# A four-layer graph network on one core: the engines' order by a list scheduler in the kernel, softmax in blocks of rows, scores as columns

## The chip, the cores and the metric

The kernel runs on one core of one Trainium2 chip. Five engines of the core matter here: TensorE (PE, matrix products and transposes, its weight loads shown apart as PEld), VectorE (DVE), ScalarE (ACT), GpSimd (POOL) and SyncE (SP, which here only issues transfers). The metric is the device time of one launch in microseconds (us), the median of three runs.

## The reference, cut to what matters

The input `x` holds 32 batches of 512 nodes by 128 features in float32; `adj` is one 512x512 matrix of zeros and ones that all batches and layers share. Four layers follow each other, each on the layer-normalised input with a residual:

```
for layer in (L0, L1, L2, L3):
    x = x + layer(relu(layernorm(x)))

L0: h = x @ Wo ; u1 = h @ a1 ; u2 = h @ a2
    e[i,k] = leaky(u1[idx1[i,k]] + u2[idx2[i,k]], 0.1)   # the indices of pairs are fixed
    att = softmax(where(adj > 0, e, -9e15), axis=1) ; out = att @ h + x @ Ws
L1: h = x @ Wp + bp ; s = leaky(h@a_src [:,None] + h@a_dst [None,:], 0.2)
    hg = relu(ln(softmax(where(A > 0, s, lowest)) * A @ h, g, b))
    z = relu(ln(((1 + eps) * hg + A @ hg) @ W1 + b1, mg, mb)) ; out = relu(z @ W2 + b2 + hg)
L2: h = x @ W ; e = leaky(h@a1 [:,None] + h@a2 [None,:], 0.2)
    out = elu(softmax(where(adj > 0, e, -9e15)) @ h + bias)
L3: A = softmax(where(adj > 0, e[cumsum index], -9e15))  # the same for every batch
    out = (A * I) @ (x @ W0) + (A * (1 - I)) @ (x @ W1) + bias
```

## The kernel before, in words

Everything stays in SBUF: `xs` holds all 32 batches (as 128 partitions by four chunks of 128 features each), loaded by SP `AHEAD = 8` batches ahead and overwritten by each layer's residual sum. One batch of one layer is a *chain*, written as a generator: `layer0` (L561), `layer1` (L636), `layer2` (L694), `layer3` (L713). A `yield` stands wherever the chain would wait. `interleave` (L40) steps through all chains that are under way, one stretch between two yields of each in turn, and lets a new one in after a number of steps, so that about `DEPTH = 6` are under way at a time. The generator `prepare` (L243), which makes what the later layers need once (score weights, centred weights, bias terms as bf16 triples, the transposed adjacency with 1 + eps on its diagonal, layer 3's softmax), is put in after two chains. The order on each engine follows from this program order and from which tile is free: scratch tiles come from pools (`wk` 18, `hp` 4 for projections, `yp` 3 for the 512x512 scores, `bg` 2 for transposed scores), and PSUM has 8 banks of 128x512.

All layers begin with `preln`: eight small statistics instructions on DVE, a power on POOL, four normalising instructions on POOL, then four PE transposes and a ReLU on ACT (`hT`, L464/466). `project_scored` (L493/497) multiplies by a weight with score columns appended (`w0_ext` 130 wide, `w1_ext` and `w2_ext` 129 wide) and copies the result to SBUF on ACT (`h_sc`).

Layers 1 and 2 share `attend` (L507). The row of neighbour scores, needed on every partition, comes from one 512-wide matmul with a weight whose score vector is repeated 128 times (`prow`, L512), so it needs only `hT`, not the projection. Four fused instructions on DVE add the mask and give the row maximum (`y`, `rmax`, L517), two small ones the shift `nmax`; ACT does the leaky ReLU (L529) and the exponential with its row sum (L530) for each block of 128 rows; after a `yield`:

```
for jb in range(C):
    pt = bank("pt")
    for ib in range(C):
        nc.tensor.transpose(pt[:, ib, :], y[:, ib, blk(jb)], ident)
```

A block of *columns* is transposed here (L539), so the first needs all four row blocks. The copies out of PSUM (`pT`) are on ACT and DVE alternately in layer 2 (L541, L543) and are DVE products with `adjT` in layer 1 (L545). Then sixteen 128x128 matmuls (`po`, L550).

Layer 0 works on transposed scores over half the nodes. After the projection, four small SP transfers gather the pair scores (`u`, L575), DVE makes `ls` (L568, L570) and `lt` (L579), PE spreads `ls` by four transposes (`repeated`, L504), DVE masks it (`y`, L588) and makes `top`, `nmax`, `ltn` (L595 to L601); ACT exponentiates (L604, L607); DVE makes `rs` and two scaled copies of h (L614 to L621); twenty matmuls (L626, L628) and the residual sum (L633) end it. Layer 1 goes on after `po` with a layer norm (POOL power L443), `hn` on DVE and POOL, the ReLU `hg` (L657, DVE), `pg` (L661, four 512-wide matmuls), `pz`, a second layer norm, transposes, `px` (L476) and two DVE instructions. Layer 2 ends with an elu (`em` L707 on ACT, then two on DVE, the last the sum into `xs`, L710). Layer 3 multiplies `hT` by one weight (`p`, L476), copies it (`h`, L724, ACT), takes the diagonal part (`own`, L717), does twenty matmuls (`po`, L728 and L732), adds and stores.

Of the kernel before, what the change touches and what calls it, by code (L numbers as in the profile page):

```python
# [23 lines left out]
F32 = mybir.dt.float32  # L25
# [5 lines left out]
P = 128  # L31
# [3 lines left out]
DEPTH = 6  # L35
# [4 lines left out]
def interleave(chains):  # L40


    waiting = list(chains)[::-1]
    running = []
    until = 0.0
    while waiting or running:
        if until <= 0.0 and waiting:
            chain, gap = waiting.pop()
            running.append(chain)
            until += gap  # L50
        until -= 1.0
        for chain in list(running):
            try:
                next(chain)
            except StopIteration:
                running.remove(chain)
# [3 lines left out]
def kernel(  # L60
# [33 lines left out]
    P1 = P + 1  # L94
# [3 lines left out]
    assert F == P and C == 4 and NE % P == 0 and B >= DEPTH  # L98
# [3 lines left out]

    def bank(name):
        return ps.tile([P, C, P], F32, tag="bank", name=name)
# [7 lines left out]


    W_O, W_S, W_P, W_1, W_2, W_L2, W_30, W_31 = range(8)
    wts = cp.tile([P, 8, P], F32, name="wts")
    att = cp.tile([P, 2], F32, name="att")
    a2 = cp.tile([P, 2], F32, name="a2")
    a1 = cp.tile([P, 3], F32, name="a1")
    e_col = cp.tile([P, KE], F32, name="e_col")
    e_last = cp.tile([P, 1], F32, name="e_last")  # L120
    eps_bc = cp.tile([P, 1], F32, name="eps_bc")
    mlp_gb = cp.tile([P, 2], F32, name="mlp_gb")
    G_G, G_B, B_2, B_L2, B_L3, B_P, B_1 = range(7)
    rows = cp.tile([P, 7, P], F32, name="rows")
    xs = cp.tile([P, B, C, P], F32, name="xs")

    bias = cp.tile([P, C, N], F32, name="bias")

    nc.scalar.dma_start(wts[:, W_O, :], l0_wo)
    nc.scalar.dma_start(att, l0_att.rearrange("(t p) o -> p (t o)", p=P))  # L130
    nc.scalar.dma_start(wts[:, W_S, :], l0_ws)
    for ib in range(C):
        nc.sync.dma_start(bias[:, ib, :], adj[blk(ib), :])

    def load_x(b):
        nc.sync.dma_start(xs[:, b], x[b].rearrange("(c p) f -> p c f", p=P))

    for b in range(AHEAD):
        load_x(b)
    for n, w in enumerate((l1_wp, l1_w1, l1_w2, l2_w, l3_w[0], l3_w[1])):  # L140
        nc.sync.dma_start(wts[:, W_P + n, :], w)
    nc.sync.dma_start(a2, l2_a.rearrange("(t p) o -> p (t o)", p=P))
    for n, v in enumerate((l1_asrc, l1_adst, l1_bp)):
        nc.sync.dma_start(a1[:, n : n + 1], v.rearrange("(p o) -> p o", o=1))
    nc.sync.dma_start(e_col, l3_e.rearrange("o (t p) -> p (o t)", p=P))
    nc.sync.dma_start(e_last, l3_e[:, NE - 1 : NE].to_broadcast([P, 1]))
    nc.sync.dma_start(eps_bc, l1_eps.rearrange("(a o) -> a o", o=1).to_broadcast([P, 1]))
    for n, v in enumerate((l1_mg, l1_mb)):
        nc.sync.dma_start(mlp_gb[:, n : n + 1], v.rearrange("(p o) -> p o", o=1))
    for n, v in enumerate((l1_gg, l1_gb, l1_b2, l2_bias, l3_bias, l1_bp, l1_b1)):  # L150
        nc.sync.dma_start(rows[:, n, :], v.rearrange("(o h) -> o h", o=1).to_broadcast([P, P]))


    ident = cp.tile([P, P], F32, name="ident")
    make_identity(nc, ident)
    mhalf = cp.tile([P, C], F32, name="mhalf")
    nc.vector.memset(mhalf, -0.5)
    minus1 = cp.tile([P, 1], F32, name="minus1")
    nc.vector.memset(minus1, -1.0)

# [43 lines left out]
    def score_weights(wn, a_cols, col, rep_src=None, rep=None):  # L204
# [8 lines left out]
        if rep is None:  # L213
            return
# [567 lines left out]
```

## Time and profile before

| what | value |
|---|---|
| median of three runs (lowest to highest) | 1177.77 us (1177.34 to 1178.57) |
| the profiled execution, its span, mean granted clock | 1178.93 us, 1177.1 us, 0.986 |
| PE `po` L550, 2048 matmuls | 243.8 us busy, mean 276 ns |
| PE `pg` L661, 256 matmuls 512 wide | 115.2 us busy, mean 592 ns |
| DVE `y` with `rmax` L517, 256 | 163.3 us busy, mean 685 ns |
| ACT `y` L529 and L530, 256 each | 167.8 and 181.9 us busy, means 717 and 715 ns |
| POOL `rstd` L443, 192 | 197.9 us busy, mean 1031 ns |
| loads of `xs`, 32 on SP | 256 KB each, 5.5 us from issue to landing |
| loads of `u`, 128 on SP | 0.5 KB each, 1.8 us |

The profile is one execution taken by the hardware. A row such as `L550 PE MATMUL po<-h_sc,pT` names the line of the kernel, the engine, the operation, the tile written and the tiles read; the first number is the busy time of all of them, the second the mean of one. Matmuls are pipelined, so the mean of one (276 ns) is longer than the distance between two starts, and the price of a matmul has to be read from such distances. The chain of waits is followed back from the last instruction: at each step to what released it. Idle time of an engine that is not the bottleneck costs nothing.

### The profile page before, as it was taken

Reading aid. Unit: us, or ns where it says so; the run is one execution under the profiler, and the core shown is the slowest. Engines: PE = TensorE matmul, PEld = TensorE weight load, DVE = VectorE, ACT = ScalarE, POOL = GpSimd, SP = SyncE. Lnnn points to the kernel's source line nnn. Section 1 sums busy time; section 2 is a strip of 40 time slices with the busy share of each in tenths; the row PEclk is TensorE's granted clock in tenths of the full one; section 3 lists DMA queues with packets and bytes.
Section 4 is the critical chain, followed back from the end, with each engine's and each line's share of the span. In section 5 each row is a group of like instructions: output and inputs, shape, how many; then the busy total and the mean of one; then the engine's idle time right before and its main releaser. Section 6 shows DMA issues by size and latency. Waiting matters only on the chain.

```text
span 1177.1 us, 24854 instructions
## 1 busy us (share of the span) xinstructions
PE 1127.4 (96%) x8543; PEld 997.1 (85%) x8543; DVE 913.5 (78%) x3918; ACT 667.3 (57%) x1588; POOL 633.3 (54%) x1008
## 2 busy tenths in 40 slices
PE   4699999999999999999999999989999999999998
PEld 3588899998788887888887888978888889999998
DVE  6879987777888888888888888999989896444221
ACT  1325554545655665555655657799999993111111
POOL 4543344450555555555555556655646557776761
PEclk8789999999999999999999999999999999999999
DMA  6800000000000000000000000000000000111111
GB/s 140 217 2 1 2 2 2 2 2 2 1 1 1 2 1 1 2 1 1 1 2 1 1 1 1 1 2 1 2 1 1 2 2 19 46 46 46 46 45 45
DMA packets 56909, 20.47 MB, mean 17 GB/s; under 512 B 21584, under 2 KB 56272, under 8 KB 56784
## 3 DMA queue, kind: packets, MB, share of 16 engines
q1 hardware_dynamic: 56224, 18.76, 6.8%
q8 instruction: 67, 1.10, 0.4%
q14 instruction: 58, 0.48, 0.1%
q10 hardware_dynamic: 560, 0.13, 0.1%
HBM read 10.43 MB, written 8.39 MB: 16 GB/s over the span
## 4 chain that ended last, share of the span: by engine, by line
PE 71%; ACT 11%; DVE 11%; DMA 3%; SPq 2%; issue 2%; POOL 0%; DVEq 0%; ACTq 0%; POOLq 0%
PE po L550 14%; PE po L732 10%; PE pg L661 9%; PE pt L539 7%; PE po L628 5%; PE proj L493 5%; ACT y L530 4%; PE prow L512 3%; PE pt L464 3%; ACT y L529 3%; PE pz L476 2%; PE p L476 2%; PE po L728 2%; PE px L476 2%; ACT y L607 2%
## 5 line engine op out<-in xcount | busy, mean ns | idle before, releaser
L443 POOL TENSOR_TENSOR rstd<-ve,mhalf 128x4 f32<-128x4 f32 x192 | 197.9, 1031 | 145.6 <-DVE ve L646 135.0
L458 POOL TENSOR_SCALAR xn<-xs,nmean,rstd 128x128 f32<-128x128 f32 x512 | 236.8, 474 | 20.6 <-PE pt L464 6.4
L550 PEld LDWEIGHTS po<-h_sc,pT 128*128 128x128 f32 x2048 | 236.4, 192 | 10.7 <-issue 5.5
L550 PE MATMUL po<-h_sc,pT 128*128 128x128 f32 x2048 | 243.8, 276 | 1.7 <-DVE pT L543 1.0
L529 ACT ACTIVATE y<-y,h_sc 128x512 f32<-128x512 f32 x256 | 167.8, 717 | 51.8 <-DVE rmax L517 49.3
L530 ACT ACTIVATE y<-y,nmax 128x512 f32<-128x512 f32 x256 | 181.9, 715 | 18.6 <-DVE nmax L525 18.5
L517 DVE CUSTOM_DVE_ANT_0 y<-prow,bias 128x512 f32<-128x512 f32 x256 | 163.3, 685 | 10.9 <-PE prow L512 10.8
L497 ACT COPY h_sc<-proj 128x258 f32<-128x258 f32 (+1 forms) x192 | 69.3, 374 | 141.5 <-PE proj L493 130.7
L451 POOL TENSOR_SCALAR ve<-mv 128x4 f32<-128x4 f32 x128 | 25.9, 203 | 223.6 <-DVE mv L438 135.9
L732 PE MATMUL po<-h,offT 128*128 128x128 f32 x1024 | 138.3, 278 | 0.9 <-ACT h L724 0.5
L539 PE MATMUL pt<-ident,y 128*128 128x128 f32 x1024 | 129.1, 275 | 4.8 <-ACT y L530 4.2
L732 PEld LDWEIGHTS po<-h,offT 128*128 128x128 f32 x1024 | 124.5, 192 | 6.7 <-ACT h L724 6.7
L539 PEld LDWEIGHTS pt<-ident,y 128*128 128x128 f32 x1024 | 113.3, 141 | 19.5 <-ACT y L530 14.7
L436 DVE BATCH_NORM_STATS2 st<-xs 128x6 f32<-128x128 f32 x512 | 119.4, 281 | 5.9 <-DMA xs<-in_x_dram 5.0
L493 PE MATMUL proj<-w_ext,hT 128*128 128x129 f32 (+1 forms) x768 | 108.3, 279 | 7.3 <-ACT hT L466 7.2
L661 PE MATMUL pg<-adjTe,hg 128*128 128x512 f32 x256 | 115.2, 592 | 0.0
L717 DVE SCALAR_TENSOR_TENSOR own<-pt,adiag_rep 128x512 f32<-128x512 f32 x32 | 22.1, 691 | 113.2 <-ACT hT L466 113.2
L493 PEld LDWEIGHTS proj<-w_ext,hT 128*128 128x128 f32 x768 | 97.2, 193 | 13.6 <-ACT hT L466 11.1
L724 ACT COPY h<-p 128x512 f32<-128x512 f32 x32 | 18.7, 586 | 155.3 <-PE p L476 155.3
L607 ACT ACTIVATE y<-y,nmax 128x256 f32<-128x256 f32 x128 | 63.5, 497 | 58.0 <-DVE nmax L598 57.9
L466 ACT ACTIVATE hT<-pt 128x512 f32<-128x512 f32 x128 | 76.7, 599 | 20.8 <-PE pt L464 19.7
L661 PEld LDWEIGHTS pg<-adjTe,hg 128*128 128x128 f32 x256 | 46.3, 190 | 46.4 <-issue 46.4
(186 smaller groups left out, 2199.1 us busy)
## 6 DMA issues: line engine op xcount, KB each, us to landing
xs<-in_x_dram SPq DMA_DIRECT2D x32, 256.0 KB, 5.5
out_dram<-yo SPq DMA_DIRECT2D x32, 256.0 KB, 2.3
u<-h_sc SPq DMA_DIRECT2D x128, 0.5 KB, 1.8
bias<-in_adj_dram SPq DMA_DIRECT2D x4, 256.0 KB, 5.3
wts<-in_L_gnn_W_dram SPq DMA_DIRECT2D x5, 64.0 KB, 3.7
rows<-in_L_gnn_b_dram SPq DMA_DIRECT2D x2, 64.0 KB, 7.4
rows<-in_L_gnn_bias_dram SPq DMA_DIRECT2D x2, 64.0 KB, 6.7
wts<-L_gnn_others_weight_dram ACTq DMA_DIRECT2D x1, 64.0 KB, 2.9
```

The costliest lines, as they stand in the source:

```text
L436: nc.vector.bn_stats(st[:, c, :], src[:, c, :])
L443: nc.gpsimd.tensor_tensor(rstd, ve, mhalf, ALU.pow)
L458: nc.gpsimd.tensor_scalar(xn[:, c, :], src[:, c, :], nmean[:, c : c + 1], rstd[:, c : c + 1], ALU.add, ALU.mult)
L493: nc.tensor.matmul(pt[:, c, :], lhsT=hT[:, blk(2 * k + c)], rhs=w_ext, start=(b3 is None), stop=(b3 is None or c == 1),)
L517: nc.vector.tensor_tensor_reduce(y[:, ib, :], wide(prow), bias[:, ib, :], 1.0, LOWEST, ALU.add, ALU.max, rmax[:, ib : ib + 1],)
L529: nc.scalar.activation(y[:, ib, :], y[:, ib, :], AF.Prelu, alpha=0.2, bias=h[:, ib, P:P1])
L530: nc.scalar.activation(y[:, ib, :], y[:, ib, :], AF.Exp, bias=nmax[:, ib : ib + 1], accum_out=ssum[:, ib : ib + 1],)
L539: nc.tensor.transpose(pt[:, ib, :], y[:, ib, blk(jb)], ident)
L550: nc.tensor.matmul(po[:, ib, :], lhsT=pT[:, jb, blk(ib)], rhs=h[:, jb, 0:P], start=(jb == 0), stop=(jb == C - 1),)
L607: nc.scalar.activation(y[:, jb, :], y[:, jb, :], AF.Exp, bias=nmax[:, jb : jb + 1], accum_out=ssum[:, jb : jb + 1],)
L661: nc.tensor.matmul(wide(pg), lhsT=hg[:, nb, :], rhs=adjTe[:, nb, :], start=(nb == 0), stop=(nb == C - 1))
L732: nc.tensor.matmul(po[:, ib, :], lhsT=offT[:, jb, blk(ib)], rhs=h1[:, jb, :], start=False, stop=(jb == C - 1),)
```

## The change

Three things change at once. First, the generators and `interleave` go. Each layer now states its operations to a `Plan`: the engine, an assumed length in us, what it reads and writes. `Plan.run` simulates the engines with those lengths and an assumed delay per engine, and picks, step by step, the operation that can begin first; among those of an engine that can begin within `SLACK` of each other, the one with the smallest `turn` (the chain's planned begin plus four times the way that the operation has behind it in its chain). At most `WINDOW = 7` chains are open. Each instruction is then tied to the previous one of its engine, so that every engine keeps to the planned order. Scratch tiles and PSUM banks are rooms of that simulation. `prepare` is a *filler*: its turn is behind all others, and it takes a bank only if two others stay free.

Second, `attend` transposes a block of *rows* as soon as that block's exponential is done, copies it and multiplies it, so that each of the four blocks goes through by itself. In layer 2 one of the four copies is on ACT instead of two.

Third, in layers 1 and 2 both scores are appended to the projection as columns (`w1_ext` and `w2_ext` are 130 wide), and `prow` is four transposes of the neighbour column repeated along the free dimension, taken after the projection's copy.

Along with it: layer 1's `hg` ReLU is on ACT instead of DVE, layer 2's last sum on POOL instead of DVE; layer 0's small DVE steps are grouped into operations that stay together (`emit_ls`, `emit_lt`, `emit_top`, `emit_rs`, one instruction fewer), its edge counts come from sixteen one-column bf16 matmuls instead of three DVE reductions, and batch 0 of `x` is loaded ahead of the adjacency. The diff, cut to its core (unchanged lines and the restating of each layer as operations left out):

```diff
-DEPTH = 6
+WINDOW = 7
+PE, DVE, ACT, POOL, SP, ACTQ = "PE", "DVE", "ACT", "POOL", "SP", "ACTQ"
+DELAY = {PE: 0.25, DVE: 0.15, ACT: 0.2, POOL: 0.15, SP: 2.2, ACTQ: 2.2}
+SLACK = 0.05
+STRETCH = 4.0
+FILLED = 1e6
-def interleave(chains):
...
+class Room:
+    def __init__(self, count, make, reserve=0):
+        self.make, self.reserve = make, reserve
+        self.free = [0.0] * count
...
+    def chain(self, gap=0.0, filler=False):
+        self.chains.append([0, filler, FILLED if filler else self.begin])
+        self.begin += gap
+    def op(self, engine, length, emit, reads=(), writes=(), load=0.0):
...
+        needs = {}
+        for v in reads:
+            needs.update(dict.fromkeys(v.writers))
+        for v in writes:
+            needs.update(dict.fromkeys(v.writers))
+            needs.update(dict.fromkeys(v.readers))
+        for v in reads:
+            v.readers.append(op)
+        for v in writes:
+            v.writers.append(op)
+        for n in needs:
+            n.after.append(op)
+            if n.chain == k:
+                op.way = max(op.way, n.way + n.length + DELAY[n.engine])
+        op.turn = (self.chains[k][2] + STRETCH * op.way, len(self.ops))
+        op.missing = len(needs)
+        self.chains[-1][0] += 1
+        self.ops.append(op)
+    def run(self):
...
+            best = None
+            for engine, ops in ready.items():
+                could = []
+                for op in ops:
+                    k = op.chain
+                    filler = self.chains[k][1]
+                    if not filler and order[k] >= oldest + WINDOW:
+                        continue
+                    begin = max(idle[engine], op.ready)
+                    new = [s for s in op.slots if s.tile is None]
+                    rooms = {}
+                    for s in new:
+                        rooms[s.room] = rooms.get(s.room, 0) + 1
+                    for room, n in rooms.items():
+                        if len(room.free) < n + (room.reserve if filler else 0):
+                            begin = None
+                            break
+                        begin = max(begin, sorted(room.free)[n - 1])
+                    if begin is not None:
+                        could.append((begin, op.turn, op))
+                if could:
+                    first = min(c[0] for c in could)
+                    c = min((c for c in could if c[0] <= first + SLACK), key=lambda c: c[1])
+                    if best is None or c[0] < best[0]:
+                        best = c
+            assert best is not None, "no operation can begin"
+            begin, _, op = best
+            ready[op.engine].remove(op)
+            for s in op.slots:
+                if s.tile is None:
+                    s.room.free.remove(min(s.room.free))
+                    s.tile = s.room.make(s.name)
+            end = begin + op.length
+            idle[op.engine] = end
+            done = end + DELAY[op.engine]
+            if op.load:
+                bus = max(done, bus) + op.load
+                done = bus
+            op.emit()
+            traced = nc.cur_bb.bb.instructions
+            while seen < len(traced):
+                ins = traced[seen]
+                seen += 1
+                if ins.engine in last:
+                    tc.add_manual_dep(
+                        ins, last[ins.engine].name,
+                        mybir.DependencyInfo(mybir.DependencyClass.NoSync, mybir.DependencyReason.DATA),
+                        reason="the plan's order",
+                    )
+                last[ins.engine] = ins
+            left[op.chain] -= 1
+            for s in op.slots:
+                s.users -= 1
+                s.until = max(s.until, done)
+                if not s.users:
+                    s.room.free.append(s.until)
+            for n in op.after:
+                n.missing -= 1
+                n.ready = max(n.ready, done)
+                if not n.missing:
+                    ready[n.engine].append(n)
...
+    banks = Room(8, lambda n: ps.tile([P, C, P], F32, tag="bank", name=n), reserve=2)
+    by_pool = room("by_pool", 5, (P, C, P))
+    by_act = room("by_act", 6, (P, C, P))
+    by_dve = room("by_dve", 5, (P, C, P))
+    scored = room("scored", 5, (P, C, P2))
+    scores = room("scores", 8, (P, C, P))
+    turned = room("turned", 4, (P, C, P))
+    spare = room("spare", 9, (P, C, P))
...
+    load_x(0)
+    for ib in range(C):
+        load(SP, lambda ib=ib: bias[:, ib, :], adj[blk(ib), :], [v_adj[ib]], 1.0)
+    for b in range(1, AHEAD):
+        load_x(b)
+    load(ACTQ, lambda: wt_o.t[:, 0, :], l0_wo, [wt_o], 0.25)
+    load(ACTQ, lambda: att, l0_att.rearrange("(t p) o -> p (t o)", p=P), [v_att])
+    load(ACTQ, lambda: wts[:, W_S, :], l0_ws, [v_wts[W_S]], 0.25)
+    v_w0b = Value()
+    score_weights(lambda: wt_o.t[:, 0, :], wt_o, att, v_att, w0_ext[:, P:P2], v_w0)
...
     def attend(...)
-        prow = bank("prow")
-        nc.tensor.matmul(wide(prow), lhsT=rep, rhs=hT, start=True, stop=True)
+        prow = repeated(lambda k: h[0].t[:, k, P + 1 : P2], h)
...
+        po = parts(banks, "po", C)
+        for ib in range(C):
+            def emit_leaky(ib=ib):
+                yw = wide(y[ib].t)
+                nc.scalar.activation(yw, yw, AF.Prelu, alpha=0.2, bias=h[0].t[:, ib, P : P + 1])
+            op(ACT, 0.61, emit_leaky, h, [y[ib]])
...
+            op(ACT, 0.7, emit_exp, [nmax], [y[ib], ssum[ib]])
+            pt = value(banks, "pt")
+            turn_op(lambda k, pt=pt: pt.t[:, k, :], lambda k, ib=ib: y[ib].t[:, k, :], [y[ib]], [pt])
+            if weights is not None:
+                pT = value(turned, "pT")
+                op(DVE, 0.6, lambda ib=ib, pt=pt, pT=pT: nc.vector.tensor_mul(pT.t, pt.t, weights[:, :, blk(ib)]),
+                   [pt, *v_weights], [pT])
+            elif ib == 0:
+                pT = value(by_act, "pT")
+                copy_op(ACT, 0.49, lambda pT=pT: pT.t, lambda pt=pt: pt.t, [pt], [pT])
+            else:
+                pT = value(turned, "pT")
+                copy_op(DVE, 0.6, lambda pT=pT: pT.t, lambda pt=pt: pt.t, [pt], [pT])
+            def emit_po(ib=ib, pT=pT):
+                for jb in range(C):
+                    nc.tensor.matmul(
+                        po[ib].t[:, ib, :], lhsT=pT.t[:, jb, :], rhs=h[0].t[:, jb, 0:P],
+                        start=(jb == 0), stop=(jb == C - 1),
+                    )
+            op(PE, 0.9, emit_po, [pT, *h], [po[ib]])
+        return po, ssum
...
     def layer0(b)
+        hT, _ = preln(b)
+        if b + AHEAD < B:
+            load_x(b + AHEAD)
+        h = project_scored(hT, w0_ext, [v_w0, v_w0b])
...
+        def emit_pair():
+            u.own = small("u", (P, H, 2))
+            for k in range(2):
+                for up in range(2):
+                    nc.sync.dma_start(
+                        u.own[up * 64 : up * 64 + 64, :, k : k + 1], h[0].t[k:P:2, up:C:2, P + k : P + k + 1]
+                    )
+        op(SP, 1.8, emit_pair, h, [u])
+        def emit_ls():
+            sc = small("sc")
+            nc.vector.tensor_add(sc, h[0].t[:, :, P], h[0].t[:, :, P + 1])
+            ls.own = small("ls")
+            nc.vector.scalar_tensor_tensor(ls.own, sc, 0.1, sc, ALU.mult, ALU.max)
+        op(DVE, 0.16, emit_ls, h, [ls])
...
+        def emit_lt():
+            lt1 = small("lt1", (P, H))
+            nc.vector.tensor_add(lt1, u.own[:, :, 0], u.own[:, :, 1])
+            lt.own = small("lt", (P, 2, H))
+            lt1_2 = lt1.rearrange("p (o h) -> p o h", o=1).to_broadcast([P, 2, H])
+            nc.vector.scalar_tensor_tensor(lt.own, lt1_2, 0.1, lt1_2, ALU.mult, ALU.max)
+            lt.less = small("ltm")
+            nc.vector.scalar_tensor_tensor(lt.less, wide(lt.own), -1.0, maxbT, ALU.mult, ALU.subtract)
+        op(DVE, 0.25, emit_lt, [u, v_cnt], [lt])
+        nmax = Value()
+        def emit_top():
+            nmax.own = small("nmax")
+            nc.vector.scalar_tensor_tensor(nmax.own, rmax.own, -1.0, lt.less, ALU.mult, ALU.min)
+            nmax.ltn = small("ltn")
+            nc.vector.tensor_add(nmax.ltn, wide(lt.own), nmax.own)
+            nc.vector.tensor_scalar(nmax.ltn, nmax.ltn, 0.0, None, ALU.min)
+        op(DVE, 0.25, emit_top, [*top, lt], [nmax])
+        e2 = Value()
...
+        def emit_rs():
+            s2 = small("s2")
+            nc.vector.tensor_mul(s2, e2.own, cnt2T)
+            rs.own = small("rs")
+            nc.vector.tensor_add(rs.own, s2, ssum[0].own)
+            nc.vector.reciprocal(rs.own, rs.own)
+            rs.second = small("rs2")
+            nc.vector.tensor_mul(rs.second, rs.own, e2.own)
+        op(DVE, 0.4, emit_rs, [e2, *ssum, v_cnt], [rs])
+        op(DVE, 0.6, lambda: nc.vector.tensor_mul(hs.t, h[0].t[:, :, 0:P], per_chunk(rs.own)), [rs, *h], [hs])
+        op(DVE, 0.6, lambda: nc.vector.tensor_mul(hs2.t, h[0].t[:, :, 0:P], per_chunk(rs.second)), [rs, *h], [hs2])
...
     def layer1(b)
-        nc.vector.tensor_scalar(hg, hn, 0.0, None, ALU.max)
+        op(POOL, 1.25, lambda: nc.gpsimd.tensor_add(hn.t, hn.t, row_of(G_B)), [v_rows], [hn])
+        hg = value(by_act, "hg")
+        op(ACT, 0.61, lambda: nc.scalar.activation(hg.t, hn.t, AF.Relu), [hn], [hg])
     def layer2(b)
-        nc.vector.scalar_tensor_tensor(xs[:, b], em, -1.0, xs[:, b], ALU.add, ALU.add)
+        op(POOL, 1.25, lambda: nc.gpsimd.tensor_add(xs[:, b], xs[:, b], em.t), [em], [v_x[b]])
...
-    chains.insert(2, (prepare(), 1.0))
-    interleave(chains)
+    plan.chain(filler=True)
+    prepare()
+    for layer, gap in ((layer0, 6.6), (layer1, 13.3), (layer2, 7.6), (layer3, 5.9)):
+        for b in range(B):
+            plan.chain(gap)
+            layer(b)
+    plan.run()
```

## The prediction

> **What bounds the kernel now.** I read the page first (busy shares and slices), then the chain that ended last, stage by stage, then busy time by stretches, then single timelines.
>
> ```profile
> PE 1127.4 (96%) x8543; PEld 997.1 (85%) x8543; DVE 913.5 (78%) x3918; ACT 667.3 (57%) x1588; POOL 633.3 (54%) x1008
> 20.00:30.00 10.00, 6.29 (x26) 5.47 (x26) 7.64 (x32) 0.97 (x2) 4.03 (x9) 0.50 0.39 45
> 30.00:40.00 10.00, 3.08 (x14) 2.53 (x12) 8.13 (x65) 3.33 (x13) 3.11 (x6) 0.50 0.74 185
> 310.00:690.00 380.00, 380.00 (x2599) 309.94 (x2598) 328.59 (x1370) 223.72 (x476) 215.68 (x310) 1.00 0.01 1
> 800.00:900.00 100.00, 98.93 (x781) 88.20 (x780) 92.47 (x336) 99.25 (x227) 57.15 (x92) 1.00 0.01 1
> ```
>
> The rows with two times are stretches: length, then busy PE, PEld, DVE, ACT, POOL, then granted clock, DMA share, GB/s. PE is nominally full nearly everywhere, but each layer has its own bound. The chain shows it:
>
> ```profile
> 313.23 0.86 PE prow L512 x2
> 314.09 3.57 PE po L550 x32
> 317.66 3.44 PE pg L661 x8
> ...
> 323.07 1.75 PE pt L539 x16
> ...
> 336.68 1.75 PE pt L539 x16
> ```
>
> Layer 1 is PE without a hole: the same piece returns after 13.61 us. From it come PE's true prices, start to start: a 128x128 f32 matmul 0.223 (3.57/16), a transpose 0.109 (1.75/16), the 512-wide `prow` 0.86.
>
> ```profile
> by line: ACT y L607 33.0%; DVE y L588 19.2%; DVE hs L621 9.3%; DVE xs L633 8.6%; issue 6.0%; DVE hs L619 4.1%; DVE rs L615 2.1%; DVE rs L614 2.0%; ACT e L604 1.9%; DVE rs L617 1.9%; DVE lt L579 1.5%; DVE mv L438 1.5%; DVE top L597 1.4%; DVE
> 218.52 1.48 ACT y L607 x6
> 225.38 1.49 ACT y L607 x6
> by line: ACT y L530 35.2%; ACT y L529 24.5%; ACT pT L541 10.0%; ACT h_sc L497 9.1%; issue 8.1%; ACT hT L466 6.7%; ACT em L707 6.7%
> ```
>
> Layer 0 (205 to 240 us) goes in a circle between DVE and ACT, 6.86 us a batch; layer 2 (840 to 860 us) is ACT alone, 12 batches in 96 us, 8.0 each. Layer 3 repeats `p` every 6.07 us.
>
> PE work, from these prices: layer 0 eight transposes, four projections, twenty matmuls, 6.24; layer 1 13.6; layer 2 0.44+0.89+0.86+1.75+3.57 = 7.51; layer 3 0.44+0.89+4.46 = 5.79. Times 32: 1061. `prepare` and the start add 28 (16 wide `pg`/`pd` at 0.86, `pn` 3.4, `pb` 4.4, 44 transposes, small ones 1.5). So of the span of 1177.1 some 88 us are lost: 51 before layer 1's first `po` at 291.9 (241 of work done by then), none in layer 1, 16 in layer 2 (0.49 x 32), 9 in layer 3 (0.28 x 32), 4 after the last matmul, 8 at the crossings.
>
> **The change part by part.**
>
> Scores as columns. 64 times a 512-wide matmul (0.86) becomes four transposes; layer 0's `prow` L504 starts at 233.56 and the next piece at 234.00, so 0.44. PE loses 0.42 x 64 = 27 us. Bounds: the transposes' listed 0.60 would save 17, nothing would save more than 27. The second score column costs nothing visible (258 to 260 wide: copies of 374 and 375 ns). `prow` now waits for the ACT copy of h; other chains cover that. The sixteen one-column `counts` matmuls add 2 (16 loads at 98 ns to `pn`'s 0.21 each: 1.6 to 3.4); they replace three DVE reductions of 4.7. PE work becomes 1089 - 27 + 2 = 1064. What follows is what is lost around it.
>
> Start and layer 0: 24 lost (now some 41 by 90 us, 51 by 292). On SP's queue the first `u` now stands behind eighteen 256 KB loads (0.97 us each on SP before) and nine small ones: issued near 20, landing near 25. Before, it was issued at 23.34, the third `u` stood behind fifteen more loads (34.70, 12.80 us), and PE did 3.1 of 10 us at 30 to 40. Afterwards only one load stands between two `u`, 2.8 us of SP against 6.2 of PE. x of batch 0 goes ahead of adjacency, so DVE starts near 5 instead of 8.9. Seven chains get as far as `prow` meanwhile (1.8 of PE each); PE has done 16 when the first `po` can start near 31, so 15 are lost. From there DVE sets the pace, because dependent small operations now stand back to back:
>
> ```profile
> 233.54 0.19 DVE L614 TENSOR_TENSOR rs<-s,ssum 128x4 f32<-128x4 f32 x1 [1.28 <-ACT y L607]
> 233.76 0.18 DVE L615 RECIPROCAL rs<-rs 128x4 f32<-128x4 f32 x1
> 233.97 0.16 DVE L617 TENSOR_TENSOR rs<-rs,e 128x4 f32<-128x4 f32 x1
> 234.06 0.68 DVE L619 TENSOR_TENSOR hs<-h_sc,rs 128x512 f32<-128x512 f32 x1
> ```
>
> Dependent ones start 0.21 apart, independent ones 0.09. Per batch: statistics 1.32, `ls` 0.29, `rmax` 4 x 0.345, `lt` 0.49, `top` 0.49, `rs` 0.69, two `hs` 1.2, the add 0.6: 6.46, above PE's 6.24, while the plan's table has 5.5. DVE's 207 plus 19 of masks and layer 1's first statistics, from 5 us, with 3% of waits, end layer 0 near 235, with 211 of PE work done: 24. Bounds 14 (PE never waits after 31) and 37 (6.86 as now). [...]
>
> Crossing into layer 1: 14. `prepare` is a filler that needs free banks and `spare` tiles, and its order on DVE is bunched after the last layer 0 add: two centred rows, `eye_e`, `wT`, four `num`, w1_ext, bp_c, then two chains of seven dependent steps for the bias terms (2.0 each), some 13 us, plus 2.7 of waiting for `pb` (4.4). Every layer 1 projection waits for both bias terms: near 18 us after the last `po`; through copy, `prow`, `rmax`, exp and the first pT its first `po` comes some 30 us after. PE has 21 us of counted work in that time (`pn`, `pb`, seven projections, transposes); 9 are lost, and some 5 more while DVE's 6.9 a chain meets 5.3 of PE up to the first `pg`. Bounds 0 (now `prepare` lies beside layer 0) and 27 (nothing overlaps). The stretches at 20 to 40 show clock 0.50 where PE is busy a third to two thirds. [...]
>
> Layer 1: 5. PE 13.18, DVE now about 12.2 (11.8 less `hg`'s 0.40, which goes to ACT, plus six dependent steps). It ran with no loss at DVE 86%; at 93% I take 0.15 a batch; bounds 0 and 0.49, layer 2's loss now. Between layers 1 and 2: 3, bounds 0 and 8.
>
> Layer 2: 16. Blocks: one pT copy of four on ACT instead of two, 8.0 - 0.48 = 7.52 (two copies, started 0.96 apart from what follows). DVE gets that copy (0.61) and gives the last add (0.61) to POOL (1.28, as `v` L703; POOL then has 5.6 and is hidden). PE 7.09, DVE 7.4, ACT 7.5: I take 7.6, so 0.51 x 32. Bounds 14 and 29 (no gain). Earlier starts of transposes are worth nothing where ACT is full.
>
> Crossing into layer 3: 7. The last part of `prepare` (four exps, 7.8 us of DVE division and diagonal, five transposes, copies) now follows layer 2's last exps; the first layer 3 `po` waits for offT and adiag_rep, 13 us after the last pT, with 6 of PE work beside. Bounds 0 and 13. Layer 3: 2 (`po` now stands behind other work, not behind its own h copy; bounds 0 and 9). End: 5.
>
> Sum: 1064 + 24 + 14 + 5 + 3 + 16 + 7 + 2 + 5 = 1140 of span. The profiled execution was 1178.93 for 1177.1, and 1.2 above the median of the three runs, so **1140 us** again.
>
> **The rivals.**
>
> Covered order (0.22): DVE's dependent steps and both crossings find cover. Losses 14 + 3 + 0 + 1 + 14 + 2 + 0 + 5 = 39: 1103. For: layer 1's clean PE; against: DVE's 6.46 and the order of `prepare`.
>
> DVE-bound crossing (0.15): layer 0 stays at 6.86 (37) and the crossings cost 22 and 12: 1166. For: the circle in layer 0's chain, the half clock at 20 to 40.
>
> Head of the queue (0.11, ends slower): in layer 1 an engine held to its order waits for one late operand and everything behind it waits too; 12.2 of DVE in 13.18 leave 1 us to recover in. Each 0.1 us a batch costs 3.2; past 1.2 us a batch more (14.5) the kernel is slower than before. At 15.0, 1140 + 32 x 1.67 = 1193. Against: now layer 1 loses nothing, and seven chains are in flight.
>
> No saving from the columns is excluded by L504's 0.44.
>
> **How the numbers follow.** The forecast holds 0.52. For 8 in 10, leaving out the slower rival and the covered one's lower half: 1104 to 1172. Faster by over 0.2% (about what a measurement can tell here): forecast, covered and DVE-bound cases, 0.87 with some of their tails beyond 1175 taken off, 0.86; within it 0.02; slower 0.12.
>
> **What would show it.** Right: `prow` groups of four transposes and none 512 wide; layer 1 returning every 13.2 to 13.5; DVE, not ACT, in layer 0's chain, near 6.6; a stretch of 10 to 20 us near 235 with PE half empty and a lower clock, DVE full of `prepare`; layer 2 near 7.6; a hole before layer 3's first `po`. Wrong: layer 0 at 6.25, no hole near 235, or layer 1 above 14.

## The result

The changed kernel takes 1182.26 us (1180.77 to 1182.39, five runs) against 1177.61 for the kernel before in the same session: a ratio of 1.0036, 95% interval 1.0021 to 1.005. It is slower by a third of a per cent, where 1140 was forecast, and outside the range of 1104 to 1172. The profiled execution has a span of 1180.3 us at a mean clock of 0.975 (0.986 before). The variants below were timed in three later sessions, in which the kernel before took 1177.98, 1176.85 and 1177.74 us, so their differences from 1182.26 are good to about 1 us. One of the four runs of e8, at a clock of 0.558, took 1890.87 us and is left out of its number.

The page's line of busy shares, after:

```profile
PE 1109.0 (94%) x8682; PEld 1002.6 (85%) x8683; DVE 961.3 (81%) x3854; ACT 665.4 (56%) x1588; POOL 670.2 (57%) x1040
```

PE's busy time fell by 18 us, so work did leave PE; DVE's rose by 48, though it has fewer instructions. Added up one by one, DVE's instructions last 1211 us after the change and 1212 before; what grew is the time that they cover, because fewer of them overlap. Busy time by stretches, after (length, then busy PE, PEld, DVE, ACT, POOL, then granted clock, DMA share, GB/s):

```profile
20.00:30.00 10.00, 5.89 (x22) 4.42 (x23) 9.01 (x58) 2.09 (x5) 9.49 (x19) 0.56 0.34 74
30.00:40.00 10.00, 7.60 (x52) 6.97 (x50) 9.14 (x51) 6.84 (x26) 8.27 (x17) 0.84 0.13 10
243.00:280.00 37.00, 24.70 (x144) 20.43 (x144) 26.51 (x92) 15.95 (x38) 4.90 (x10) 0.78 0.00 1
310.00:690.00 380.00, 376.58 (x2643) 308.18 (x2643) 335.74 (x1331) 229.86 (x497) 219.34 (x299) 1.00 0.00 1
800.00:900.00 100.00, 90.98 (x789) 89.39 (x790) 95.33 (x311) 93.33 (x211) 68.35 (x102) 0.98 0.00 1
977.00:993.00 16.00, 7.98 (x33) 5.35 (x32) 15.55 (x51) 4.52 (x8) 11.66 (x14) 0.61 0.00 1
1000.00:1150.00 150.00, 149.71 (x1343) 149.52 (x1342) 69.28 (x277) 29.02 (x50) 106.20 (x177) 1.00 0.16 47
```

There are two new holes in PE, from 243 to 280 and from 977 to 993, both with a lowered clock (0.78 and 0.61), and at 800 to 900 PE is at 91% where it was at 99%, while DVE is at 95%. The chain by line of the two windows shown before, 205 to 240 and 840 to 860:

```profile
by line: PE po L749 66.4%; PE po L741 16.9%; PE pt L375 6.7%; PE proj L544 5.1%; PE prow L375 5.1%
...
by line: PE po L624 26.6%; DVE pT L368 15.0%; DVE y L574 12.0%; DVE v L829 10.3%; PE proj L544 8.9%; DVE st L461 8.8%; DVE nmean L489 6.2%; DVE mv L463 4.3%; DVE em L837 3.0%; issue 2.0%; DVE rs L828 0.9%; DVE top L585 0.9%; DVE nmax L587 0
```

Layer 2 was ACT's alone; now most of its chain is DVE. In layer 0 the chain names PE, not DVE as the prediction's sign had it, and PE counts as busy for 99.7 of the 100 us from 100 to 200. Even so DVE sets the pace there: a batch returns every 6.43 us, 0.2 above PE's 6.24, and DVE, busy for 94.0 of those 100 us with short gaps between dependent steps, waits for another only once, for 0.2 us. This is all that the view of DVE's waits from 100 to 200 has:

```profile
DVE lt L683 <- DMA u<-h: 0.2, 1, 0.2
```

To compare with the prediction's ledger, the matmuls of a stage are summed at the start-to-start prices that the prediction gives (0.223 for a 128x128 f32 matmul, which the profile shows as two halves, 0.109 a transpose, 0.86 for a 512-wide one); the time of the stage beyond that sum is lost.

| stage | predicted lost | measured lost |
|---|---|---|
| PE work itself | 1064 | 1061 |
| start and layer 0 (first matmul at 12.8, end 242) | 24 | 39 |
| crossing into layer 1 (to 300) | 14 | 22 |
| layer 1 and into layer 2 (to 719) | 5 + 3 | 10 |
| layer 2 (719 to 977) | 16 | 29 |
| crossing into layer 3 (977 to 993) | 7 | 13 |
| layer 3, end | 2 + 5 | 3 + 4 |
| sum | 1140 | 1180 |

(The span is 1180.3; the rounded terms add up to 1181.) Work went as forecast. The start with layer 0, both crossings and layer 2 lost 42 us more than forecast, three of the four at their upper bounds (37, 29 and 13); the rest lost about what was forecast.

The crossing into layer 1, in pieces of the chain from 240 to 300, after:

```profile
250.01 0.21 DVE wT L368
...
255.72 4.28 PE pb L1032 x20
...
264.21 0.49 DVE in_row L1071
...
277.78 1.10 PE pt L375 x4
278.90 0.70 DVE pT L613
279.65 5.94 PE po L624 x32
```

`prepare` on DVE and PE, from layer 0's end to 267, then the first chain of layer 1, and its first `po` at 279.65: the hole that the forecast put near 235, some 8 us later. Layer 3's first `po` starts at 993.18, 16.5 us after layer 2's last one (976.7); in the kernel before it started 9 us ahead of layer 2's last.

### The profile page after: what moved, and what is told of

The parts are those of the page before. It is cut to its first block, busy times and chain, and to the rows that moved or that the text cites. A ratio compares the mean times of both kernels' runs of the same rounds, so it can differ in the third digit from the quotient of the medians.

```text
span 1180.3 us, 25261 instructions
## 1 busy us (share of the span) xinstructions
PE 1109.0 (94%) x8682; PEld 1002.6 (85%) x8683; DVE 961.3 (81%) x3854; ACT 665.4 (56%) x1588; POOL 670.2 (57%) x1040
## 4 chain that ended last, share of the span: by engine, by line
PE 60%; DVE 28%; ACT 4%; POOL 3%; issue 2%; DMA 2%; SPq 0%; DVEq 0%; ACTq 0%; POOLq 0%
PE po L624 11%; PE po L860 10%; PE pt L375 7%; PE po L749 7%; PE pg L795 6%; DVE y L574 5%; PE proj L544 4%; DVE st L461 4%; DVE pT L368 3%; PE po L856 2%; PE p L522 2%; DVE pT L613 2%; ACT y L604 2%; PE prow L375 2%; PE px L522 2%
## 5 line engine op out<-in xcount | busy, mean ns | idle before, releaser
L624 PE MATMUL po<-h,pT 128*128 128x128 f32 x2048 | 249.5, 278 | 17.3 <-DVE pT L368 14.3
L624 PEld LDWEIGHTS po<-h,pT 128*128 128x128 f32 x2048 | 239.6, 194 | 26.1 <-DVE pT L368 17.6
L596 ACT ACTIVATE y<-y,h 128x512 f32<-128x512 f32 x256 | 165.5, 718 | 48.6 <-DVE rmax L574 48.4
L795 PE MATMUL pg<-adjTe,hg 128*128 128x512 f32 x256 | 126.2, 593 | 0.0
L544 PE MATMUL proj<-w_ext,hT 128*128 128x130 f32 x768 | 110.2, 283 | 2.0 <-ACT hT L506 1.9
L366 ACT COPY h<-proj 128x260 f32<-128x260 f32 x192 | 66.7, 370 | 79.6 <-PE proj L544 63.2
L461 DVE BATCH_NORM_STATS2 st<-xs 128x6 f32<-128x128 f32 x512 | 110.6, 277 | 0.3 <-DMA xs<-in_x_dram 0.3
L613 DVE TENSOR_TENSOR pT<-pt,adjT 128x512 f32<-128x512 f32 x128 | 81.3, 680 | 15.5 <-PE pt L375 15.3
L375 PE MATMUL pt<-ident,xn 128*128 128x128 f32 x512 | 86.0, 283 | 5.5 <-POOL xn L497 3.9
L375 PEld LDWEIGHTS pt<-ident,xn 128*128 128x128 f32 x512 | 63.4, 143 | 21.8 <-POOL xn L497 16.2
```

The costliest lines, as they stand in the source:

```text
L375: nc.tensor.transpose(dst(k), src(k), ident)
L461: nc.vector.bn_stats(st[:, c, :], src(c))
L544: nc.tensor.matmul(p[:, c, :], lhsT=column(hT, 2 * k + c), rhs=w_ext, start=(b3 is None), stop=(b3 is None or c == 1),)
L596: nc.scalar.activation(yw, yw, AF.Prelu, alpha=0.2, bias=h[0].t[:, ib, P : P + 1])
L613: op(DVE, 0.6, lambda ib=ib, pt=pt, pT=pT: nc.vector.tensor_mul(pT.t, pt.t, weights[:, :, blk(ib)]), [pt, *v_weights], [pT])
L624: nc.tensor.matmul(po[ib].t[:, ib, :], lhsT=pT.t[:, jb, :], rhs=h[0].t[:, jb, 0:P], start=(jb == 0), stop=(jb == C - 1),)
```

## The experiments

### First four: prepare early, columns undone, columns alone, the first loads

Theory A put the loss down to the place of `prepare`; B to the columns; C to an order that every engine is held to and that was planned with wrong lengths.

**e1**, `prepare` early:

```diff
-FILLED = 1e6
+FILLED = 60.0
```

> The changed kernel with one constant different: the one-time preparation (prepare) gets the priority of a chain that begins at 60 us of the plan instead of a priority behind all other work; it stays a filler otherwise. Theory A (the place of prepare): the changed kernel loses 17 us of PE between 243 and 280, 5 up to 300, about 8 in the first third of layer 2 and 11 between 977 and 993 because prepare's DVE work was left to the end of the layer before; moved into layer 0 it costs that layer about 12 (DVE 205 + 35 of prepare against PE 200 + 28). Time about 1150, layer 1's first po near 262, no hole before layer 3's first po. Theory B (the columns give their gain back in waits) and theory C (every engine held to an order that was planned with wrong lengths loses a little everywhere): the holes at the crossings move into layer 0 and only there, time 1170 or more.

Measured: 1168.48 us, 0.9922 of the kernel before (0.9902 to 0.9942), 13.8 less than the changed kernel. Half of A holds. The hole before layer 3 is gone: its first `po` (967.3) starts before layer 2's last (987.8). But layer 1's first `po` comes at 288.6, 9 us later than before the edit, not at 262. In layer 0, stretches of e1:

```profile
100.00:120.00 20.00, 17.34 (x99) 12.48 (x98) 18.86 (x80) 6.72 (x24) 3.30 (x6) 0.91 0.11 26
120.00:140.00 20.00, 17.61 (x123) 14.38 (x122) 19.07 (x85) 7.23 (x25) 8.42 (x12) 1.00 0.13 28
```

DVE is at 94 and 95%, PE at 87 and 88%. A layer that DVE fills has no room for `prepare`; the loss moved.

**e2**, the score columns undone in the changed kernel:

```diff
-        prow = repeated(lambda k: h[0].t[:, k, P + 1 : P2], h)
+        prow = value(banks, "prow")
+        op(PE, 0.86, lambda: nc.tensor.matmul(
+            wide(prow.t), lhsT=wrep, rhs=wide(hT.t), start=True, stop=True), [hT, v_wrep], [prow])
...
+        copy_op(DVE, 0.15, lambda: w1_rep, lambda: w1_ext[:, P + 1 : P2].to_broadcast([P, P]), [], [v_w1])
```

> The changed kernel with the score columns undone: prow is one 512-wide matmul with a weight repeated 128 times again, and needs only hT. PE work grows by 64 x 0.42 = 27 us. Theory A: the columns are worth their price where PE sets the pace (layer 1, 13.5 us) and little where DVE does (layer 2, 7.75 a batch against PE's 7.09): time about 1196. Theory B: what the columns save is lost again because prow now waits for the projection's copy on ACT: time 1182 or less. Theory C: as A.

Measured: 1204.26 us (1.0226, 1.0202 to 1.0249). In this order the columns are worth 22.0 us of the 27 that they take off PE. B falls.

**e3**, the columns alone, in the kernel before:

```diff
-        prow = bank("prow")
-        nc.tensor.matmul(wide(prow), lhsT=rep, rhs=hT, start=True, stop=True)
+        yield
+        prow = repeated(h[:, :, P1])
...
-        for layer, steps in ((layer0, 9), (layer1, 18), (layer2, 11), (layer3, 6))
+        for layer, steps in ((layer0, 9), (layer1, 19), (layer2, 12), (layer3, 6))
```

> The kernel before with only the score columns changed: w1_ext and w2_ext 130 wide, prow by four transposes of the projected column, one yield more in attend; order, softmax and everything else as before. Theory A: layer 1 is PE alone and returns every 13.2 instead of 13.61 (13.5 us), layer 2 is ACT alone at 8.0 and gains nothing: time about 1164. Theory B: the wait for the copy of h breaks the clean cycle of layer 1: time 1176 or more.

Measured: 1208.19 us (1.0261, 1.0233 to 1.029), 30 slower than before, not 14 faster. Layer 1's `po` no longer returns every 13.61 us but every 13.2, 17.4, 11.9, 15.8, 13.9, 13.2 in turn, 14.2 in the mean. What PE waited for from 310 to 690 in e3 (in the kernel before this view has no line):

```profile
PE po L548 <- DVE pT L543: 11.4, 6, 2.4
PE proj L491 <- ACT hT L464: 4.3, 4, 1.1
PE pt L462 <- POOL xn L456: 1.0, 1, 1.0
```

The loss is not layer 1's alone: counted as in the ledger, e3 loses 35 us from the first `po` of layer 1 to its last `pg` (1 before) and 37 from there to layer 2's last `po` (16 before).

So the same columns cost 30 us in the generators' order and bring 22 in the planned one. Another place of the yields might cost less; one was tried. And the rest of the change without the columns (e2 against the kernel before) costs 26. Neither of the two parts pays by itself; row blocks alone were not tried.

**e4**, layer 0's weight first on SP:

```diff
+    load(SP, lambda: wt_o.t[:, 0, :], l0_wo, [wt_o], 0.25)
+    load(SP, lambda: att, l0_att.rearrange("(t p) o -> p (t o)", p=P), [v_att])
     load_x(0)
...
-    load(ACTQ, lambda: wt_o.t[:, 0, :], l0_wo, [wt_o], 0.25)
-    load(ACTQ, lambda: att, l0_att.rearrange("(t p) o -> p (t o)", p=P), [v_att])
```

> The changed kernel with layer 0's weight and attention vector loaded first on SP instead of on ACT's queue, where the weight's load is issued at 7.95 us (0.78 before) because the ninth load waits for an earlier one to land. If that load is what holds up the start: first matmul near 8 instead of 12.8, first po of layer 0 near 33 instead of 39.5, time about 1176. If the start hangs on the order of DVE's statistics and the pair scores instead: first po stays beyond 37 and the time within 2 us of 1182.

Measured: 1181.58 us, the same as the changed kernel (1182.26). The first matmul moves from 12.8 to 3.0 and the first `po` from 39.5 to 36.5, but layer 0 ends at 240.9 instead of 242.0. What DVE waited for from 24 to 44 in e4:

```profile
DVE lt L683 <- DMA u<-h: 6.7, 3, 3.4
```

What is won at the first matmul is lost again to the pair scores, which stand on SP behind other loads (in e4 SP issues almost without a gap from 28.35 to 33.49, two loads among the pair scores, and the last of these takes 2.95 us to land). In the changed kernel itself DVE has nothing to do for 7.68 us at the start, because the next instruction of its order needs that weight:

```profile
12.69 0.23 DVE L368 COPY w_ext<-wt_o 128x128 f32<-128x128 f32 x1 [7.68 <-DMA wt_o<-L_gnn_others_weight_dram]
```

### Second four: less work on DVE

Theory D, from e1: DVE sets the pace of layers 0 and 2, and `prepare` adds to it wherever it lies.

**e5**, no negated mean on DVE:

```diff
-                    xn.t[:, c, :], src[:, c, :], nmean.own[:, c : c + 1], rstd.own[:, c : c + 1],
-                    ALU.add, ALU.mult,
+                    xn.t[:, c, :], src[:, c, :], mv.own[:, c, 0:1], rstd.own[:, c : c + 1],
+                    ALU.subtract, ALU.mult,
```

> The changed kernel without the DVE instruction that negates the mean in every layer norm: POOL's normalising instruction subtracts the mean itself. Takes 128 instructions of 0.17 to 0.65 us (33.7 us) off DVE and nothing else. Theory D (after the first four runs): DVE sets the pace of layer 0 (6.46 a batch) and of layer 2 (7.8 a batch), so time follows DVE's work there: layer 0 near 6.25, layer 2 near 7.5, time about 1167. Theory C (the losses come from an order held to that was planned with wrong lengths, whatever DVE's load): within 3 us of 1182.

Measured: 1248.18 us, 66 slower than the changed kernel. It tells nothing on D, because another thing changed: POOL's normalising instruction, a group of e5,

```profile
L491 POOL TENSOR_SCALAR xn<-xs,mv,rstd 128x128 f32<-128x128 f32 x512 | 421.1, 833 | 31.4 <-DVE yo L861 25.9 <-PE pt L375 0.5
```

took 462 ns in the changed kernel and takes 833 here. POOL's instructions add up to 880 us here, against 670 busy in the changed kernel; that POOL became the bound is an estimate from these sums. Whether the subtraction does it or the mean read with a stride of two was not separated.

**e6**, the small steps apart (one of five such places):

```diff
-        def emit_ls():
-            sc = small("sc")
-            nc.vector.tensor_add(sc, h[0].t[:, :, P], h[0].t[:, :, P + 1])
-            ls.own = small("ls")
-            nc.vector.scalar_tensor_tensor(ls.own, sc, 0.1, sc, ALU.mult, ALU.max)
-        op(DVE, 0.16, emit_ls, h, [ls])
+        def emit_sc():
+            sc.own = small("sc")
+            nc.vector.tensor_add(sc.own, h[0].t[:, :, P], h[0].t[:, :, P + 1])
+        def emit_ls():
+            ls.own = small("ls")
+            nc.vector.scalar_tensor_tensor(ls.own, sc.own, 0.1, sc.own, ALU.mult, ALU.max)
+        op(DVE, 0.09, emit_sc, h, [sc])
+        op(DVE, 0.09, emit_ls, [sc], [ls])
```

> The changed kernel with the grouped small DVE steps of layer 0 (emit_ls, emit_lt, emit_top, emit_rs) and of attend (emit_top) given to the plan one instruction at a time, so that others can come between dependent ones. Same instructions. Theory D: dependent ones stand 0.21 apart and others 0.09, eight pairs a batch in layer 0: its DVE falls from 6.46 to about 5.5 and PE sets the pace at 6.3; layer 2 gains 0.1 a batch; time about 1171. Theory C, or if the plan keeps them together anyway: within 3 us of 1182.

Measured: 1158.83 us (0.9848, 0.9833 to 0.9862): 23.4 less than the changed kernel with the same instructions. The three steps of `lt` in DVE's timeline, first in the changed kernel:

```profile
126.80 0.15 DVE L683 TENSOR_TENSOR lt<-u 128x2 f32<-128x2 f32 x1
126.99 0.16 DVE L686 SCALAR_TENSOR_TENSOR lt<-lt 128x4 f32<-128x4 f32 x1
127.18 0.16 DVE L688 SCALAR_TENSOR_TENSOR ltm<-lt,maxbT 128x4 f32<-128x4 f32 x1
```

and in e6:

```profile
127.29 0.15 DVE L694 TENSOR_TENSOR lt<-u 128x2 f32<-128x2 f32 x1
127.36 0.17 DVE L761 RECIPROCAL rs<-rs 128x4 f32<-128x4 f32 x1
127.45 0.14 DVE L718 TENSOR_TENSOR ltn<-lt,nmax 128x4 f32<-128x4 f32 x1
127.51 0.15 DVE L699 SCALAR_TENSOR_TENSOR lt<-lt 128x4 f32<-128x4 f32 x1
```

Dependent ones start 0.19 apart; with another batch's steps between them, a start comes every 0.06 to 0.09. That agrees with the row of the kernel before that the prediction went by (0.21 and 0.09). Layer 0 goes from 6.43 to 6.23 a batch, the prediction's 6.24 of PE work, and ends at 229. DVE now waits there: of the view of its waits from 100 to 200, the first line in e6:

```profile
DVE sc L663 <- ACT h L366: 8.2, 13, 0.6
```

The losses of the start and layer 0 are 26 (39 before the edit), layer 2's 21 (29); the two crossings stay at 21 and 13. The gain is twice the 11 us that D gave for it.

**e7**, e1, e5 and e6 together:

> e1 (prepare early) with e5 and e6 on top. Theory D: in e1 prepare's DVE work only moved the loss into a layer 0 that DVE already filled (layer 1's first po at 288.6 instead of 279.6); with a lighter DVE the 45 us of prepare fit beside 228 us of PE: layer 1's first po near 265, layer 2 near 7.5, time about 1138. If the crossings cost because of prepare's own chain of waits and not because of DVE's load: layer 1's first po stays beyond 280 and the time beyond 1155.

Measured: 1212.43 us. It has e5's slow POOL instruction in it, so it decides nothing between the two cases. It is 36 less than e5, about what the same two edits bring without e5 below (e9, 35).

**e8**, layer 2's last sum on DVE again:

```diff
-        op(POOL, 1.25, lambda: nc.gpsimd.tensor_add(xs[:, b], xs[:, b], em.t), [em], [v_x[b]])
+        op(DVE, 0.6, lambda: nc.vector.tensor_add(xs[:, b], xs[:, b], em.t), [em], [v_x[b]])
```

> The changed kernel with one part undone: layer 2's last sum into xs is on DVE again (0.6 us) instead of POOL (1.25 us). Theory D: layer 2 goes from 7.8 to about 8.4 a batch, time about 1198. If POOL's sum costs DVE as much as it takes off it (nmean and nmax of layers 1 and 2 last up to 1.3 us where a 512-wide POOL sum runs beside them): layer 2 within 0.15 of 7.8, time 1178 to 1187.

Measured: 1191.69 us, 9.4 slower than the changed kernel: between the two expectations. The move to POOL takes 32 x 0.6 = 19 us off DVE and brings half of that. Where the rest goes can be seen in the changed kernel's timeline, first beside the moved sum, then beside another POOL sum of layer 2, which was on POOL before as well:

```profile
796.24 1.27 POOL L838 TENSOR_TENSOR xs<-xs,em 128x512 f32<-128x512 f32 x1 [2.30 <-DVE top L585]
796.27 1.26 DVE L587 SCALAR_TENSOR_TENSOR nmax<-top 128x4 f32<-128x4 f32 x1
848.20 1.27 POOL L832 TENSOR_TENSOR v<-v,rows 128x512 f32<-128x512 f32 x1
848.86 0.65 DVE L489 TENSOR_SCALAR nmean<-mv 128x4 f32<-128x4 f32 x1
```

DVE steps of 0.15 and 0.17 us last 1.26 and 0.65 and end at 797.53 and 849.51, with the POOL sums beside them (797.51 and 849.47). This is no chance: of the changed kernel's 128 `nmean`, 58 last over 0.2 us, and 57 of these end within 0.04 us of the end of a POOL instruction; of the other 70, none does. In all, before and after the change, and in e8:

```profile
L453 DVE TENSOR_SCALAR nmean<-mv 128x4 f32<-128x4 f32 x128 | 26.2, 205 | 1.4 <-POOL xn L458 1.3
L525 DVE SCALAR_TENSOR_TENSOR nmax<-top 128x4 f32<-128x4 f32 x64 | 9.9, 154 | 0.1
L489 DVE TENSOR_SCALAR nmean<-mv 128x4 f32<-128x4 f32 x128 | 33.7, 264 | 5.8
L587 DVE SCALAR_TENSOR_TENSOR nmax<-top 128x4 f32<-128x4 f32 x64 | 19.3, 302 | 2.2
L489 DVE TENSOR_SCALAR nmean<-mv 128x4 f32<-128x4 f32 x128 | 26.4, 206 | 5.9
L587 DVE SCALAR_TENSOR_TENSOR nmax<-top 128x4 f32<-128x4 f32 x64 | 16.2, 253 | 2.2
```

With the sum back on DVE, `nmean` is as short as before the change and `nmax` takes 3 us less in all: together 10 of the 19 us. `nmax` stays at 16.2 us, against 9.9 before the change, so undoing the moved sum takes back 3.1 of the 9.4 us that it grew by; where the other 6.3 come from was not tried. In the changed kernel 10 of the 64 `nmax` last over 0.2 us, and all 10 end within 0.04 us of the end of a POOL instruction. The profile shows the ends together (0.02 and 0.04 apart above); what holds the DVE step until then it does not show. The prediction weighed POOL's 1.28 us only against POOL's own time.

### Last four: the parts together

**e9** is e6 with e1's constant.

> The small DVE steps apart (as in e6, 1158.83) and prepare early (as in e1). Theory D: in e6 layer 0 is PE's (6.23 a batch), so prepare's DVE work now fits beside it: layer 1's first po at 262 to 272 (266.7 in e6), and the hole of 16.5 us between layer 2's last po and layer 3's first one goes, as it did in e1: time about 1142. If prepare's own chain of dependent steps holds up layer 0's order on each engine whatever DVE's load: layer 1's first po beyond 280, time 1152 or more.

Measured: 1147.30 us (0.974, 0.9724 to 0.9756). Layer 1's first `po` is at 264.0, before layer 0's end, and layer 3's (947.7) before layer 2's last. D holds, though the gain is 5 us short of its number.

**e10** is e6 with the negated mean on POOL:

```diff
-            nc.vector.tensor_scalar(nmean.own, mv[:, :, 0], -1.0, None, ALU.mult)
-        mv = variances(lambda c: src[:, c, :], [v_x[b]], minus_mean, 0.1)
+        mv = variances(lambda c: src[:, c, :], [v_x[b]])
...
+            nc.gpsimd.tensor_scalar(nmean.own, mv.own[:, :, 0], -1.0, 0.0, ALU.mult, ALU.add)
+        op(POOL, 0.2, minus_mean, [mv], [nmean])
```

> e6 with the negated mean of every layer norm made by a POOL instruction (0.2 us) instead of a DVE one (37.1 us in all in e6); unlike in e5 the normalising instruction stays as it was, addition and product. Theory D: layer 0 is PE's in e6 and gains nothing, layer 2 (7.72) goes to ACT's 7.5: 5 us or so, and 2 to 4 in layer 1: time about 1151. If layer 2 is held by ACT already: within 2 us of 1158.8.

Measured: 1144.80 us (0.972, 0.9706 to 0.9735), 14.0 less than e6 and more than expected. From layer 1's last `pg` to layer 2's last `po` it takes 241.3 us instead of 249.9, and ACT fills layer 2 again (busy for 99.45 of the 100 us from 800 to 900), at 7.4 a batch (7.7 in e6).

**e11** is e9 and e10 together.

> e9 and e10 together. Theory D: the two add up: time about 1135, layer 1's first po near 264, layer 2 near 7.5. Else as e9.

Measured: 1134.30 us (0.9631, 0.9617 to 0.9646); D's 1135.

**e12** splits `prepare`, so that layer 3's part lies in layer 1:

```diff
-    plan.chain(filler=True)
+    plan.chain(filler=60.0)
     prepare()
...
+        plan.chain(filler=450.0)
         e_at = offT[:, 0:KE, :]
```

> As e11, but prepare is split in two fillers: what layer 1 needs at 60 us of the plan, what only layer 3 needs (the pieces from e_at on) at 450, in layer 1, where PE is full and DVE has 1 us in 13 free. Theory D: about 17 us of DVE leave layer 0 for a place where they cost nothing: 3 to 6 us less than e11, about 1131. If DVE's work there delays layer 1's own steps, as every engine keeps to the planned order: no gain, layer 1 above 13.1 a batch.

Measured: 1130.31 us (0.9597, 0.9583 to 0.9611), 4 less than e11, as D has it. That is 47 us less than the kernel before and 52 less than the changed one. Layer 1's mean (13.96) is above the 13.1 named as the sign of the other case; it was a bad sign, since the first `po` now lies in layer 0, at 245.6. The page's line and two stretches of e12:

```profile
PE 1089.6 (97%) x8683; PEld 987.4 (87%) x8683; DVE 901.9 (80%) x3726; ACT 665.0 (59%) x1588; POOL 721.4 (64%) x1168
```

```profile
310.00:690.00 380.00, 374.70 (x2589) 302.40 (x2588) 332.06 (x1293) 230.54 (x494) 216.51 (x321) 1.00 0.00 1
800.00:900.00 100.00, 99.32 (x866) 95.94 (x865) 95.61 (x326) 100.00 (x230) 76.81 (x121) 1.00 0.01 1
```

DVE's busy time is 59 us below the changed kernel's, and layer 2 is ACT's again. The losses are now 31 in the start and layer 0 (up to 240), 16 in layer 1 (to 715), 14 in layer 2, 3 in layer 3 and 4 at the end, and nothing to speak of at the crossings.

## Why the prediction was wrong

- **PE work: right.** 1064 forecast, 1061 measured; `prow` is four transposes; the columns take 27 us off PE and 22.0 off the time here (e2). One stage of the forecast's ledger of the kernel before is off: counted again at its prices, 58 us, not 51, are lost before layer 1's first `po`, and what was put at "8 at the crossings" belongs there.
- **Start and layer 0: mis-sized, 24 against 39.** The pace was right (6.43 a batch on DVE, 6.46 forecast; dependent steps 0.19 to 0.2 apart). The failed step is "DVE starts near 5", with a first `po` near 31 and 15 us lost by then: the first `po` came at 39.5, and 27 of the 39 us are lost before it. DVE's first statistics do start at 3.65, but it is busy for only 8.7 of the first 20 us and stands still for 7.68 of them. The weight that the first matmul needs is issued on ACT at 7.95 us, where the kernel before has 0.78, since in the changed program its issue waits for an earlier load, which lands at 7.92. e4 shows that this load is not the whole of it: without it, the pair scores on SP hold DVE up. A slip in the sum made the term smaller still: 226 us of DVE work with 3% of waits, from 5 us on, end at 238, not 235, which is 27 lost by the forecast's own figures.
- **Crossing into layer 1: mechanism right, 22 against 14.** The place, the bunched `prepare`, the empty half of PE and the lowered clock (0.78) are as told. The cause named, free banks and `spare` tiles, is not the main one: one constant, the filler's turn, moves `prepare` (e1). By the planner's code an operation ranked last is not chosen while another can begin as early on its engine, and DVE was full.
- **Layer 1 and into layer 2: 10 against 5 and 3.** The mean period is 13.0, but uneven, with `po` distances from 7.3 to 25.4 us; which step makes it uneven was not tried. The rival of the queue's head at 15 a batch did not come.
- **Layer 2: the step that failed with it, 29 against 16.** "DVE 7.4, ACT 7.5: I take 7.6". DVE needs 7.75 in the last two thirds of the layer, in part because DVE's own small steps last longer beside POOL's sums, the moved one among them (with it back on DVE, in e8, `nmean` takes 26.4 us in all instead of 33.7). Against PE's 7.09 this makes 21 of the 29. The other 8 fall near the layer's start, where `prepare` takes 12.5 us of DVE's time between 720 and 800, which the forecast has nowhere in this layer; that these 8 are `prepare`'s was not tried by itself. From layer 1's last `pg` to layer 2's last `po` the changed kernel needs 257.7 us (719.0 to 976.7), the kernel before 255.5 (730.3 to 985.8). So the whole gain forecast for this layer (0.4 x 32) is missing. Taking small gaps (e6) and `nmean` (e10) from DVE brought it back to 241.3.
- **Crossing into layer 3: 13 against 7**, as told, at its upper bound; e1 and e12 take it away.

The second rival (DVE-bound crossing, 1166) had these numbers nearly right: 37 for the start and layer 0 (39 measured), 22 and 12 for the crossings (22 and 13). With layer 2's extra 13 it is close to the result. For layer 0 that was luck: its 37 stood for a pace of 6.86 a batch, and the pace was 6.43; the loss lay in the start. What was wrong in the reckoning is that the bounds of the terms were taken as if each could fall by itself. The crossings and layer 2 have one cause in the main, a DVE that is full (e1, e6, e9, e10), and came out high together; the range left no room for that. An order that every engine is held to does not by itself make the kernel slower than it was: with the same planner and window, small steps apart, `prepare` earlier and lighter work on DVE, it gives 1130. What the plan would give if the engines were not held to it was not tried.

## What to carry to other kernels

A planner that keeps engines to an order exposes how operations are grouped: dependent small steps given to it as one piece started 0.19 us apart here, where a start came every 0.06 to 0.09 with other steps between them; giving them apart brought 23 us. Add the work per engine and layer, with the longer DVE steps beside POOL's sums in it (17 us over `nmean` and `nmax` here), before one-time work is placed: put it where that engine has time to spare, not where the list has a gap. And losses that hang on one engine go up and down together, so their bounds add up.

## Not expected of the hardware

- The score columns cost 30 us in the kernel with the generators' order (e3) and brought 22 in the planned one (e2).
- POOL's `tensor_scalar` with a subtraction and a mean read at a stride took 833 ns, with an addition and a dense operand 462 (e5).
- DVE steps of 0.15 to 0.17 us lasted up to 1.27 us beside 128x512 sums on POOL: `nmax` of layers 1 and 2 took 9.4 us more than before the change (19.3 against 9.9), `nmean` 7.5 (33.7 against 26.2).
